# Another order inside the blocks of a fused attention and FFN layer: two chunks' float16 products together, gate ahead of value

## The chip, the cores and the metric

The kernel runs on one core of a Trainium2 chip. The metric is the device time of one execution in microseconds (us); where several executions were timed, the median is given. One execution was also recorded by the hardware profiler. The engines are named as the profile names them: PE (TensorE, matmuls), PEld (its weight loads), DVE (VectorE), ACT (ScalarE), POOL (GpSimd) and SP (SyncE, which only issues transfers here).

## The reference

The layer has 4 x 2048 = 8192 tokens of 256 features, in float32:

```python
Q, K, V = x @ W_q.T, x @ W_k.T, x @ W_v.T
S = (Q_c @ K_c.T) * mask            # in chunks of 32 tokens; mask[i, j] = decay**(i-j) for i >= j
O = S @ V_c
gate = sigmoid(x @ W_g.T)
a = (gate * O) @ W_o.T + x
h = layernorm(x + a)
u = silu(h @ wg.T) * (h @ wu.T)     # wg, wu: 768 x 256 integers / 127
out = layernorm(h + u @ wd.T)       # wd: 256 x 768 integers / 127
```

## The kernel before

The tokens are cut into 16 blocks of 512 (`TB`). One turn of the main loop, `for b in range(NB - 2)`, does the FFN of block b and, between its parts, attention of the blocks after it: `y`, the scores, gate and value of block m = b + 3, and the attention output `o` of block n = b + 2. The order on every engine is written out by hand: `in_turn` (and `in_steady_turn`) keep an instruction in the program's order on its engine. An engine runs its queue in that order; where an instruction waits, everything behind it waits too.

Products are split for precision. Of a projection on attention's side, both operands are cut into float32r pieces, and `three` makes the product in three passes: `hi` x `hi`, then `lo` x `lo` into the same PSUM bank, then ACT scales that bank in place (L542, `nc.scalar.mul(pb, pb, WHOLE)`), and only after that may the third pass, `gap` x `gap`, add to it. The passes stand at L501 where the result is feature by token (`p_y`, `p_g`; 128x512 each) and at L523 where it is token by feature (`p_v`, `p_o`; 128x256 each). The token pieces come from `pieces_of_tokens`: ACT makes `hi` (L472), POOL makes `lo` (L476), DVE makes `gap` (L481). `split_v` ends with an ACT copy of each of its two banks (L576), `split_gate` with a tanh on ACT for each (L559), `split_out` with an addition on DVE (L832).

The FFN's first half, `ffn_up`, runs over six chunks of 128 hidden features. For each it makes four products of 128x512 in float32r (`hi`: `fg_hi` and `fu_hi`, two each) and four in float16 (`lo`), all at L923; ACT takes the silu `s` of the gate bank `fg` (L932), DVE multiplies it with the bank `fu` to `u` (L943), ACT casts `u` to `u_hi` (L948) and POOL makes `u_lo` (L949). Chunks 0, 2 take `hi` first, chunks 1, 3, 4, 5 take `lo` first. With `held=True` the call returns `multiply`, so that other work can be put on the queues ahead of the multiplication.

The second half (`project_back_late`, L764) multiplies `u_hi` with `fd_hi` (float32r, 24 products of 128x256) and then `u_lo` with `fd_lo` (float16, 24). In the blocks with `late = b > 0` its products of chunks 0 and 1 stand between the second and the third pass of `split_out`:

```python
hs[n], out_rest = split_out(n, go_parts)   # passes hi and lo of o, and ACT's two scalings
...
high(range(2))                             # 8 products fdn
mv_h = out_rest()                          # pass gap of o, which needs the scalings
```

So in a block's second half PE's queue reads: chunk 4 of the FFN; value hi, lo; gate hi, lo; value gap; gate gap; chunk 5; o hi, lo; 8 products fdn; o gap; the other fdn. Beside it, in the blocks 1 to 11 (`m + 1 < NB`), the pieces of the next block's tokens are made: ACT's `x_hi` for the two halves k = 0, 1 of the features, DVE's two `x_gap`, POOL's two `x_lo`.

There are 8 PSUM banks of 128x512 float32, and a bank that was let go is taken again by a later product.

Of the kernel before, what the change touches and what calls it, by code (L numbers as in the profile page):

```python
# [58 lines left out]
TB = 512  # L59
# [17 lines left out]
def kernel(  # L77
# [18 lines left out]
    KD = D // P  # L96
# [18 lines left out]
    def in_turn(ins):  # L115
        tc.keep_in_program_order(ins)

    def bank(name):
        return psum.tile([P, TB], F32, tag="ps", name=name)
# [789 lines left out]
        while late_splits:  # L909
            late_splits.pop(0)()  # L910

    def ffn_up(b, hT, uT, chunks, cols=slice(0, TB), held=False, low_first=False):

        n = cols.stop - cols.start
        for hc in chunks:
            pg = bank(f"fg_{b}_{hc}_{cols.start}")[:, :n]
            pu = bank(f"fu_{b}_{hc}_{cols.start}")[:, :n]

            kinds = (1, 0) if hc % 2 or low_first else (0, 1)
            for kind in kinds:  # L920
                for pb, w in ((pg, fg), (pu, fu)):
                    for dc in range(KD):
                        product = nc.tensor.matmul(  # L923
                            pb,
                            lhsT=w[kind][:, dc, hc * P : (hc + 1) * P],
                            rhs=hT[kind][:, dc, cols],
                            start=(kind == kinds[0] and dc == 0),
                            stop=(kind == kinds[1] and dc == KD - 1),
                        )
                        in_turn(product)  # L930
            s = work.tile([P, n], F32, tag="s", name=f"s_{b}_{hc}")
            in_turn(nc.scalar.activation(s, pg, AF.Silu, scale=SCALE / H_UP))  # L932
            no_more_splits()
            if len(uT[0]) == hc:
                for kind, dtype, tiles in zip(("hi", "lo"), (F32R, F16), uT):
                    tiles.append(
                        acts.tile([P, TB], dtype, tag=f"u_{kind}", name=f"u_{kind}_{b}_{hc}")
                    )

            def multiply(hc=hc, pu=pu, s=s):  # L940
                u = work.tile([P, n], F32, tag="u", bufs=3, name=f"u_{b}_{hc}")
                in_steady_turn(
                    nc.vector.scalar_tensor_tensor(u, pu, U_UP / H_UP, s, ALU.mult, ALU.mult)  # L943
                )
                hi, lo = uT[0][hc][:, cols], uT[1][hc][:, cols]

                def split():
                    in_steady_turn(nc.scalar.copy(hi, u))  # L948
                    in_steady_turn(nc.gpsimd.tensor_tensor(lo, u, hi.bitcast(F32), ALU.subtract))  # L949

                if lagging:
                    late_splits.append(split)
                else:
                    split()

            if held:
                return multiply
            multiply()
# [198 lines left out]
    for b in range(NB - 2):  # L1157
        n = b + 2
        m = b + 3
        more = m < NB  # L1160
        xns[n] = load_xn(n)
        if b and m + 1 < NB:
            xTs[m + 1] = load_xT(m + 1)
        hT = hTs.pop(b)
        uT = ([], []) if b else uT_0
        sT, v, sg = ahead
        if not more:
            scales_next = iterated_scale_and_shift(mv_out, of_out, f"out_{b}")
        if b:
            normalize(hs[b + 1], *scales_h)  # L1170
            up_now(b, hT, uT, 0)
        multiply = ffn_up(b, hT, uT, range(1, 2), held=True)
        if b:
            moving = move_h(b + 1, hs[b + 1])
        else:
            cast_fd(0, range(2, 3))
            multiply()
            x_gaps()
            sT = attn_scores(n, yT)
            xTs[m + 1] = load_xT(m + 1)  # L1180
        if more:
            yT, y_rest = split_y(m, x_parts)
        if b:
            multiply()
        if not more:
            goT = attn_values(n, sT, v, sg)
        multiply = ffn_up(b, hT, uT, range(2, 3), held=True)
        if b > 1:
            normalize(r_before, *scales_out, range(NG // 2))
        multiply()  # L1190
        if more:
            y_rest()
        if b == 0:
            normalize(hs[b + 1], *scales_h)
            moving = move_h(b + 1, hs[b + 1])
        if not more:
            go_parts, go_gaps = token_parts(goT, f"go_{n}")
        multiply = ffn_up(b, hT, uT, range(3, 4), held=True)
        if b > 1:
            normalize(r_before, *scales_out, range(NG // 2, NG))  # L1200
        multiply()
        if b > 1:
            store(b - 2, r_before)
        if more:
            sT_next = attn_scores(m, yT)
            goT = attn_values(n, sT, v, sg)
            multiply = ffn_up(b, hT, uT, range(4, 5), held=True, low_first=True)
            go_parts, go_gaps = token_parts(goT, f"go_{n}")
            if b == 0:
                cast_fd(1, range(1))  # L1210
            multiply()
            go_gaps()
            v_next, v_rest = split_v(m, x_parts)
            sg_next, g_rest = split_gate(m, x_parts)
            v_rest()
            late = b > 0
            if late:
                g_rest()
                if m + 1 < NB:
                    x_parts, x_high, x_low, x_difference = pieces_of_tokens(  # L1220
                        xTs[m + 1], f"x_{m + 1}"
                    )
                    x_high(0)
                multiply = ffn_up(b, hT, uT, range(5, 6), held=True)
                if m + 1 < NB:
                    x_high(1)
                    x_difference(0)
                multiply()
                if m + 1 < NB:
                    x_difference(1)  # L1230
            else:
                if b == 0:
                    cast_fd(1, range(1, 2))
                up_with_cast(b, hT, uT, 5, 1, range(2, 3))
        else:
            up_now(b, hT, uT, 4)
            go_gaps()
        r_before = r_out
        if more:
            hs[n], out_rest = split_out(n, go_parts)  # L1240
            if b:
                hTs[b + 1] = split_h(b + 1, moving)
            begun = None
            if late:
                high, low = project_back_late(b, uT, [chunked(w) for w in fd], "fdn")
                high(range(2))
                begun = high, low, range(2, KH)
            else:
                g_rest()
            mv_h = out_rest()  # L1250
            if b == 0:
                hTs[b + 1] = split_h(b + 1, moving)
            ahead = sT_next, v_next, sg_next
            if m + 1 < NB:
                if late:
                    for k in range(KD):
                        x_low(k)
                else:
                    x_parts, x_gaps = token_parts(xTs[m + 1], f"x_{m + 1}")
            std_h = root_in_turn(mv_h, of_h, f"h_{b}")  # L1260
            if b:
                mv_before, std_before = mv_out, root_in_turn(mv_out, of_out, f"out_{b}")
            back_to_silu()

            def between():
                scales = scale_and_shift(
                    mv_h, std_h, of_h, f"h_{b}", nc.vector, in_turn
                )
                if m + 1 < NB and not late:
                    x_gaps()  # L1270
                return scales

            r_out, mv_out, scales_h = ffn_down(b, uT, hs.pop(b), between, begun=begun)
            if b:
                scales_out = scale_and_shift(mv_before, std_before, of_out, f"out_{b}")
        else:
            multiply = ffn_up(b, hT, uT, range(5, KH), held=True)
            hs[n], out_rest = split_out(n, go_parts)
            multiply()
            hTs[b + 1] = split_h(b + 1, moving)  # L1280
            scales_out = scales_next
            normalize(r_before, *scales_out)
            store(b - 1, r_before)

            def amid():
                return iterated_scale_and_shift(out_rest(), (HALF, 1.0), f"h_{n}")

            r_out, mv_out, scales_h = ffn_down(
                b, uT, hs.pop(b), chunkwise=True, amid=amid
            )  # L1290
            scales_out = iterated_scale_and_shift(mv_out, of_out, f"out_{b + 1}")
# [361 lines left out]
```

## Time and profile before

| | |
|---|---|
| time, median of 3 (range) | 485.84 us (485.81 to 486.66) |
| the profiled execution: time, span | 486.48 us, 484.8 us |
| busy: PE, PEld | 478.5 us (99%), 378.6 us (78%) |
| busy: ACT, DVE, POOL | 370.8 us (76%), 348.9 us (72%), 281.5 us (58%) |
| chain that ended last | PE 98% |
| matmuls at L923 (up) | 784, 249 us busy |
| 128x512 up products, hi / lo of fg, mean | 461 / 383 ns |
| 128x256 fdn products, hi / lo, mean | 276 / 273 ns |

Matmuls overlap: the duration of one is longer than its distance to the next one, so what PE needs for a run of products is read from the starts of successive rows and not from durations. The same holds in part for ACT and DVE, where an instruction that needn't wait starts some 0.1 us before the end of the one ahead of it. "x2" behind a row is the number of instructions merged in it, and the second number of a row is then the time from the first one's start to the last one's end.

### The profile page before, as it was taken

How to read it: one execution, taken by the hardware profiler on the slowest of the kernel's cores; microseconds unless marked ns; L12 is line 12 of the kernel's file. 1: busy time of each engine (PE TensorE's matmuls, PEld its weight loads, DVE VectorE, ACT ScalarE, POOL GpSimd, SP SyncE). 2: the span in 40 equal slices, each digit the busy share in tenths (PEclk: the TensorE clock that was granted, in tenths of full speed). 3: DMA queues.
4: the chain of work that ended last, by engine and by line, in shares of the span. 5: the costliest groups of instructions: out<-in, count | busy, mean ns of one | idle time of the engine just before them, and what ended most of it. 6: DMA issues, size and time to landing. Idle time of an engine off the chain costs nothing.

```text
span 484.8 us, 12280 instructions
## 1 busy us (share of the span) xinstructions
PE 478.5 (99%) x4760; PEld 378.6 (78%) x4760; DVE 348.9 (72%) x795; ACT 370.8 (76%) x699; POOL 281.5 (58%) x285
## 2 busy tenths in 40 slices
PE   9999999999999999999999999999999999999995
PEld 5788787787868878687787868878687787868685
DVE  4587958777677776858777677876858777577656
ACT  4778788687888788797887888788797877786845
POOL 2835755655655566455655654566455655657764
PEclk9999999999999999999999999999999999999999
DMA  8630321211313114031321313114031211103102
GB/s 258 233 96 26 112 64 46 71 62 34 105 51 119 44 41 137 25 107 49 93 79 33 108 52 117 45 45 131 26 108 50 83 45 35 56 19 114 35 16 83
DMA packets 43323, 36.99 MB, mean 76 GB/s; under 512 B 4864, under 2 KB 39168, under 8 KB 43264
## 3 DMA queue, kind: packets, MB, share of 16 engines
q1 hardware_dynamic: 42144, 35.28, 23.6%
q10 hardware_dynamic: 1120, 0.92, 0.6%
q8 instruction: 38, 0.62, 0.5%
q14 instruction: 21, 0.17, 0.1%
HBM read 20.45 MB, written 8.39 MB: 59 GB/s over the span
## 4 chain that ended last, share of the span: by engine, by line
PE 98%; DMA 1%; DVE 0%; ACT 0%; issue 0%
PE fg L923 18%; PE fu L923 18%; PE fdn L764 13%; PE p_v L523 9%; PE p_y L501 9%; PE p_o L523 9%; PE p_g L501 9%; PE po L699 4%; PE ps L663 2%; PE fdn L1001 2%; PE fdn L1395 1%; PE fdn L745 1%; PE pg L587 1%; PE pa L811 1%; PE pv L629 1%; DMA wg<-in_w_gT_dram 1%
## 5 line engine op out<-in xcount | busy, mean ns | idle before, releaser
L949 POOL TENSOR_TENSOR u_lo<-u,u_hi 128x512 f16<-128x512 f32 (+1 forms) x98 | 129.6, 1329 | 92.7 <-ACT u_hi L948 92.7
L943 DVE SCALAR_TENSOR_TENSOR u<-fu,s 128x512 f32<-128x512 f32 (+1 forms) x98 | 66.1, 675 | 46.8 <-ACT s L932 44.8
L932 ACT ACTIVATE s<-fg 128x512 f32<-128x512 f32 (+1 forms) x98 | 57.5, 587 | 34.2 <-PE fg L923 33.3
L948 ACT CAST u_hi<-u 128x512 fp32r<-128x512 f32 (+1 forms) x98 | 59.5, 607 | 31.2 <-DVE u L943 31.2
L923 PE MATMUL fg<-hT_hi,fg_hi 128*128 128x512 f32 (+1 forms) x196 | 73.1, 454 | 0.0
L923 PE MATMUL fu<-hT_hi,fu_hi 128*128 128x512 f32 (+1 forms) x196 | 60.3, 389 | 0.0
L923 PE MATMUL fg<-hT_lo,fg_lo 128*128 128x512 f16 (+1 forms) x196 | 58.2, 379 | 0.0
L923 PE MATMUL fu<-hT_lo,fu_lo 128*128 128x512 f16 (+1 forms) x196 | 57.4, 375 | 0.0
L476 POOL TENSOR_TENSOR go_lo<-goT,go_hi 128x512 fp32r<-128x512 f32 x30 | 44.6, 1506 | 18.5 <-ACT go_hi L472 18.5
L481 DVE SCALAR_TENSOR_TENSOR go_gap<-go_hi,goT 128x512 fp32r<-128x512 f32 x30 | 48.3, 1647 | 0.8 <-ACT go_hi L472 0.7
L476 POOL TENSOR_TENSOR x_lo<-xT,x_hi 128x512 fp32r<-128x512 f32 x30 | 37.6, 1273 | 15.2 <-ACT x_hi L472 15.2
L923 PEld LDWEIGHTS fg<-hT_hi,fg_hi 128*128 128x128 f32 x196 | 35.6, 190 | 10.3
L923 PEld LDWEIGHTS fu<-hT_hi,fu_hi 128*128 128x128 f32 x196 | 36.5, 188 | 8.2
L481 DVE SCALAR_TENSOR_TENSOR x_gap<-x_hi,xT 128x512 fp32r<-128x512 f32 x30 | 21.9, 740 | 27.2 <-ACT x_hi L472 27.2
L900 POOL TENSOR_TENSOR hT_lo<-hT,hT_hi 128x512 f16<-128x512 f32 x28 | 35.7, 1295 | 4.6 <-ACT hT_hi L899 4.6
L832 DVE TENSOR_TENSOR h<-p_o,x 128x512 f32<-128x512 f32 x30 | 19.3, 685 | 25.3 <-PE p_o L523 23.2
L764 PE MATMUL fdn<-fd_hi,u_hi 128*128 128x256 f32 x288 | 36.5, 276 | 0.0
L923 PEld LDWEIGHTS <-fu_lo 128*128 128x128 f16 x196 | 19.2, 98 | 22.1
L764 PEld LDWEIGHTS fdn<-fd_hi,u_hi 128*128 128x128 f32 x288 | 34.4, 188 | 0.0
L764 PE MATMUL fdn<-fd_lo,u_lo 128*128 128x256 f16 x288 | 33.5, 273 | 0.0
L923 PEld LDWEIGHTS <-fg_lo 128*128 128x128 f16 x196 | 13.2, 98 | 21.8 <-issue 16.1
L764 PEld LDWEIGHTS <-u_lo 128*128 128x128 f16 x288 | 27.2, 98 | 3.4
(179 smaller groups left out, 1065.7 us busy)
## 6 DMA issues: line engine op xcount, KB each, us to landing
x<-in_x_dram SPq DMA_DIRECT2D x16, 512.0 KB, 3.8
xT<-in_xT_dram SPq DMA_DIRECT2D x15, 512.0 KB, 4.3
hT<-sq SPq DMA_DIRECT2D x224, 32.0 KB, 1.9
out_dram<-r SPq DMA_DIRECT2D x13, 512.0 KB, 3.3
out_dram<-r SPq DMA_DIRECT2D x7, 128.0 KB, 1.7
fg_int<-in_ffn_gT_dram SPq DMA_DIRECT2D x3, 256.0 KB, 7.3
fu_int<-in_ffn_uT_dram SPq DMA_DIRECT2D x3, 256.0 KB, 6.4
fd_int<-in_ffn_dT_dram SPq DMA_DIRECT2D x3, 256.0 KB, 5.5
```

Source lines behind the costliest of these rows:

```text
L476: in_turn(nc.gpsimd.tensor_tensor(lo[:, k, :], t[:, k, :], whole, ALU.subtract))
L481: nc.vector.scalar_tensor_tensor(gap[:, k, :], whole, -WHOLE, t[:, k, :], ALU.mult, ALU.add)
L501: nc.tensor.matmul(pb, lhsT=a[kind][:, k, i * P : (i + 1) * P], rhs=b[kind][:, k, :], start=kind + k == 0, stop=True, skip_group_check=True,)
L523: nc.tensor.matmul(pb[:, j * D : (j + 1) * D], lhsT=b[kind][:, k, g * P : (g + 1) * P], rhs=a[kind][:, k, :], start=kind + k + j == 0, sto ...
L699: product = nc.tensor.matmul(po[dims, dc * len(groups) + g, :], lhsT=v[rows, g, dc * P + dims.start : dc * P + dims.stop], rhs=sT[rows, g, :],
L764: nc.tensor.matmul(banks[g // per][:, g % per * D : (g % per + 1) * D], lhsT=part[:, g * P : (g + 1) * P], rhs=w, start=first and g % per ...
L900: nc.gpsimd.tensor_tensor(in_order[1], whole, in_order[0].bitcast(F32), ALU.subtract)
L923: product = nc.tensor.matmul(pb, lhsT=w[kind][:, dc, hc * P : (hc + 1) * P], rhs=hT[kind][:, dc, cols], start=(kind == kinds[0] and dc == ...
L932: in_turn(nc.scalar.activation(s, pg, AF.Silu, scale=SCALE / H_UP))
L943: nc.vector.scalar_tensor_tensor(u, pu, U_UP / H_UP, s, ALU.mult, ALU.mult)
L948: in_steady_turn(nc.scalar.copy(hi, u))
L949: in_steady_turn(nc.gpsimd.tensor_tensor(lo, u, hi.bitcast(F32), ALU.subtract))
```

## The change

The blocks 1 to 12 get another order; block 0 and the last three are left as they were.

- Chunks 0 and 1: all eight float16 products first, then the eight float32r products.
- Chunk 3: `hi` first instead of `lo` first.
- Chunks 4 and 5: the eight float16 products together, then chunk 4's float32r ones. Chunk 5's float32r products are moved behind the gate's third pass and ahead of the value's.
- Gate is made ahead of value.
- ACT's order behind that: the two tanh, the silu of chunk 5, the two copies of `v`, both `x_high`. Then `x_difference(0)` on DVE, then chunk 5's multiplication (DVE) with its cast (ACT), then `x_difference(1)`. Before, `x_high(0)` stood ahead of that silu and `x_high(1)` behind it, and `x_difference(0)` was also ahead of the multiplication.

`ffn_up` is cut into `ffn_pieces`, which gives the float32r products, the float16 products and the activation of one chunk as three functions. The number of instructions of each kind is unchanged.

```diff
@@ -909,25 +909,30 @@
         while late_splits:
             late_splits.pop(0)()
 
-    def ffn_up(b, hT, uT, chunks, cols=slice(0, TB), held=False, low_first=False):
+    def ffn_pieces(b, hT, uT, hc, cols=slice(0, TB)):
 
         n = cols.stop - cols.start
-        for hc in chunks:
-            pg = bank(f"fg_{b}_{hc}_{cols.start}")[:, :n]
-            pu = bank(f"fu_{b}_{hc}_{cols.start}")[:, :n]
-
-            kinds = (1, 0) if hc % 2 or low_first else (0, 1)
-            for kind in kinds:
-                for pb, w in ((pg, fg), (pu, fu)):
-                    for dc in range(KD):
+        pg = bank(f"fg_{b}_{hc}_{cols.start}")[:, :n]
+        pu = bank(f"fu_{b}_{hc}_{cols.start}")[:, :n]
+        fresh = [pg, pu]
+
+        def products(kind):
+            for i, (pb, w) in enumerate(((pg, fg), (pu, fu))):
+                for dc in range(KD):
+                    for part in [cols]:
                         product = nc.tensor.matmul(
-                            pb,
+                            pb[:, part.start - cols.start : part.stop - cols.start],
                             lhsT=w[kind][:, dc, hc * P : (hc + 1) * P],
-                            rhs=hT[kind][:, dc, cols],
-                            start=(kind == kinds[0] and dc == 0),
-                            stop=(kind == kinds[1] and dc == KD - 1),
+                            rhs=hT[kind][:, dc, part],
+                            start=len(fresh) > 1 - i,
+                            stop=True,
+                            skip_group_check=True,
                         )
                         in_turn(product)
+                        if len(fresh) > 1 - i:
+                            fresh.pop()
+
+        def activate():
             s = work.tile([P, n], F32, tag="s", name=f"s_{b}_{hc}")
             in_turn(nc.scalar.activation(s, pg, AF.Silu, scale=SCALE / H_UP))
             no_more_splits()
@@ -937,7 +942,7 @@
                         acts.tile([P, TB], dtype, tag=f"u_{kind}", name=f"u_{kind}_{b}_{hc}")
                     )
 
-            def multiply(hc=hc, pu=pu, s=s):
+            def multiply():
                 u = work.tile([P, n], F32, tag="u", bufs=3, name=f"u_{b}_{hc}")
                 in_steady_turn(
                     nc.vector.scalar_tensor_tensor(u, pu, U_UP / H_UP, s, ALU.mult, ALU.mult)
@@ -953,6 +958,17 @@
                 else:
                     split()
 
+            return multiply
+
+        return lambda: products(0), lambda: products(1), activate
+
+    def ffn_up(b, hT, uT, chunks, cols=slice(0, TB), held=False, low_first=None):
+
+        for hc in chunks:
+            high, low, activate = ffn_pieces(b, hT, uT, hc, cols)
+            for products in (low, high) if (hc % 2 if low_first is None else low_first) else (high, low):
+                products()
+            multiply = activate()
             if held:
                 return multiply
             multiply()
@@ -1166,10 +1182,25 @@
         sT, v, sg = ahead
         if not more:
             scales_next = iterated_scale_and_shift(mv_out, of_out, f"out_{b}")
+        late = more and b > 0
+
+        def pieces(hc):
+            return ffn_pieces(b, hT, uT, hc)
+
         if b:
             normalize(hs[b + 1], *scales_h)
-            up_now(b, hT, uT, 0)
-        multiply = ffn_up(b, hT, uT, range(1, 2), held=True)
+        if late:
+            (high_0, low_0, silu_0), (high_1, low_1, silu_1) = pieces(0), pieces(1)
+            low_0()
+            low_1()
+            high_0()
+            silu_0()()
+            high_1()
+            multiply = silu_1()
+        else:
+            if b:
+                up_now(b, hT, uT, 0)
+            multiply = ffn_up(b, hT, uT, range(1, 2), held=True)
         if b:
             moving = move_h(b + 1, hs[b + 1])
         else:
@@ -1195,7 +1226,7 @@
             moving = move_h(b + 1, hs[b + 1])
         if not more:
             go_parts, go_gaps = token_parts(goT, f"go_{n}")
-        multiply = ffn_up(b, hT, uT, range(3, 4), held=True)
+        multiply = ffn_up(b, hT, uT, range(3, 4), held=True, low_first=not late)
         if b > 1:
             normalize(r_before, *scales_out, range(NG // 2, NG))
         multiply()
@@ -1204,33 +1235,40 @@
         if more:
             sT_next = attn_scores(m, yT)
             goT = attn_values(n, sT, v, sg)
-            multiply = ffn_up(b, hT, uT, range(4, 5), held=True, low_first=True)
-            go_parts, go_gaps = token_parts(goT, f"go_{n}")
-            if b == 0:
-                cast_fd(1, range(1))
-            multiply()
-            go_gaps()
-            v_next, v_rest = split_v(m, x_parts)
-            sg_next, g_rest = split_gate(m, x_parts)
-            v_rest()
-            late = b > 0
             if late:
+                (high_4, low_4, silu_4), (high_5, low_5, silu_5) = pieces(4), pieces(5)
+                low_4()
+                low_5()
+                go_parts, go_gaps = token_parts(goT, f"go_{n}")
+                high_4()
+                silu_4()()
+                go_gaps()
+                sg_next, g_rest = split_gate(m, x_parts)
+                v_next, v_rest = split_v(m, x_parts)
                 g_rest()
+                high_5()
+                multiply = silu_5()
+                v_rest()
                 if m + 1 < NB:
                     x_parts, x_high, x_low, x_difference = pieces_of_tokens(
                         xTs[m + 1], f"x_{m + 1}"
                     )
-                    x_high(0)
-                multiply = ffn_up(b, hT, uT, range(5, 6), held=True)
-                if m + 1 < NB:
-                    x_high(1)
+                    for k in range(KD):
+                        x_high(k)
                     x_difference(0)
                 multiply()
                 if m + 1 < NB:
                     x_difference(1)
             else:
-                if b == 0:
-                    cast_fd(1, range(1, 2))
+                multiply = ffn_up(b, hT, uT, range(4, 5), held=True, low_first=True)
+                go_parts, go_gaps = token_parts(goT, f"go_{n}")
+                cast_fd(1, range(1))
+                multiply()
+                go_gaps()
+                v_next, v_rest = split_v(m, x_parts)
+                sg_next, g_rest = split_gate(m, x_parts)
+                v_rest()
+                cast_fd(1, range(1, 2))
                 up_with_cast(b, hT, uT, 5, 1, range(2, 3))
         else:
             up_now(b, hT, uT, 4)
```

## The prediction

> **What bounds the kernel now.** First the page's head and its chain of the work that ended last, then what PE waited for between 90 and 420 us, where twelve blocks repeat every 29.07 us (in the chain's rows, value begins at 148.72 and 177.78).
>
> ```profile
> PE 478.5 (99%) x4760; PEld 378.6 (78%) x4760; DVE 348.9 (72%) x795; ACT 370.8 (76%) x699; POOL 281.5 (58%) x285
> PEclk9999999999999999999999999999999999999999
> PE 98%; DMA 1%; DVE 0%; ACT 0%; issue 0%
> ```
>
> PE is the chain, at full granted clock, and in that stretch the list of PE's waits is empty. So only two things move the time: the pace of PE's products, and a wait that PE doesn't have now. For both I read one block's second half, engine by engine. PE first (start, time from first start to last end, engine, line, product):
>
> ```profile
> 154.07 0.60 PE L923 MATMUL fg<-hT_lo,fg_lo 128*128 128x512 f16 x2
> 154.51 0.59 PE L923 MATMUL fu<-hT_lo,fu_lo 128*128 128x512 f16 x2
> 154.76 0.82 PE L923 MATMUL fg<-hT_hi,fg_hi 128*128 128x512 f32 x2
> 155.41 0.62 PE L923 MATMUL fu<-hT_hi,fu_hi 128*128 128x512 f32 x2
> 155.87 0.64 PE L523 MATMUL p_o<-wo_hi,go_hi 128*128 128x256 f32 x4
> 157.71 1.07 PE L764 MATMUL fdn<-fd_hi,u_hi 128*128 128x256 f32 x8
> 158.62 1.07 PE L523 MATMUL p_o<-wo_gap,go_gap 128*128 128x256 f32 x8
> ```
>
> The last row is the one to watch: o's third pass, which needs ACT's scaling of the bank. ACT and DVE in the same stretch:
>
> ```profile
> 152.95 1.08 ACT L576 COPY v<-p_v 128x512 f32<-128x512 f32 x2
> 153.92 1.10 ACT L559 ACTIVATE sg<-p_g 128x512 f32<-128x512 f32 x2
> 154.88 0.65 ACT L472 ACTIVATE x_hi<-xT 128x512 fp32r<-128x512 f32 x1
> 155.61 0.60 ACT L932 ACTIVATE s<-fg 128x512 f32<-128x512 f32 x1
> 156.11 0.62 ACT L472 ACTIVATE x_hi<-xT 128x512 fp32r<-128x512 f32 x1
> 157.02 0.62 ACT L948 CAST u_hi<-u 128x512 fp32r<-128x512 f32 x1 [0.29 <-DVE u L943]
> 157.55 1.06 ACT L542 ACTIVATE p_o<-p_o 128x512 f32<-128x512 f32 x2
> ...
> 155.57 0.69 DVE L481 SCALAR_TENSOR_TENSOR x_gap<-x_hi,xT 128x512 fp32r<-128x512 f32 x1 [2.47 <-ACT x_hi L472]
> 156.30 0.69 DVE L943 SCALAR_TENSOR_TENSOR u<-fu,s 128x512 f32<-128x512 f32 x1
> 156.91 0.68 DVE L481 SCALAR_TENSOR_TENSOR x_gap<-x_hi,xT 128x512 fp32r<-128x512 f32 x1
> ```
>
> The first scaling ends at 157.55 + 0.58 (a single one's length, from the p_g row below) = 158.13, and PE begins the third pass at 158.62. That 0.49 us, less what handing over takes, is all the room there is today. The scaling stands behind the cast of u, the cast behind u on DVE, and u behind the first x_gap: a queue of three engines in step.
>
> **The change, part one: fewer changes of product type on PE.** From start to start the four float16 products of one chunk go at 0.22 us each (two fg in 154.51 - 154.07 = 0.44). Float32r products inside a long run go at 0.23 (p_y, 168.04 to 169.41: six in 1.37). By ends of single products, the float16 ones are 216 ns apart and long-run float32r ones 229; the first float16 product behind float32r ends 230 behind it, 14 more than its like; four float32r ones behind float16 take 929 to 936 instead of 4 x 229 = 916, some 16 more. A switch to float16 and back therefore costs 0.030 us.
>
> Per block: with chunks 0 and 1 one switch pair goes (float16 now follows fdn's own float16): 0.030. With 4 and 5 another: 0.030. With chunk 3 hi first, its float32r joins p_y's third pass and the scores follow float16, a neighbour that no row shows; the return is saved (0.016) unless the scores pay it, so 0 to 0.03. Gate ahead of value exchanges neighbours of one type: 0, within 0.01. Sum 0.06 to 0.09, I take 0.076, times 12 blocks = 0.9 us saved.
>
> [...]
>
> **Part two: where the room goes.** Call E the end of the value's last gap product, now the last thing ahead of o. Chunk 5's float32r products stand 8 gap products (0.92 us) ahead of E, so its silu is done in time. But ACT now has four instructions between that silu and the cast, and the first two wait for the value's gap:
> - The second v copy can start at E + 0.04 (an ACT instruction follows PE by 0.04: p_g's lo ends at 152.39, its scaling starts at 152.43).
> - x_hi(0) starts 0.49 later (spacing of the pairs in the ACT rows): E + 0.53, ends at + 0.65: E + 1.18. x_hi(1) follows and is no further burden.
> - x_gap(0) on DVE 0.03 later (155.53 to 155.57): E + 1.21.
> - u of chunk 5 is behind it: 0.61 later (156.30 to 156.91): E + 1.82, ends at E + 2.51. s and fu were ready long before; it waits only for its turn.
> - u_hi 0.03 later, E + 2.54; the scaling of p_o 0.53 later (157.02 to 157.55), E + 3.07, ends at E + 3.65.
> - PE follows ACT after 0.05: E + 3.70. That spacing is from an early wait, rows below: the scalings start at 64.14, the first ends at 64.72, PE at 64.77.
>
> ```profile
> 152.43 0.58 ACT L542 ACTIVATE p_g<-p_g 128x512 f32<-128x512 f32 x1 [0.34 <-PE p_g L501]
> 64.14 1.06 ACT L542 ACTIVATE p_v<-p_v 128x512 f32<-128x512 f32 x2
> 64.77 1.22 PE L523 MATMUL p_v<-wv_gap,x_gap 128*128 128x256 f32 x8
> ```
>
> PE's own way: o's first product starts 0.16 before the end of the one ahead of it (fu_hi ends at 155.41 + 0.62 = 156.03, p_o starts at 155.87), o's 16 products take 157.71 - 155.87 = 1.84, the 8 of fdn 158.62 - 157.71 = 0.91. So PE is at the third pass at E + 2.59. It waits 3.70 - 2.59 = 1.11 us, where it had 0.49 to spare. A product that starts from a wait took 0.11 longer (387 ns at 64.77, 278 for the next), so 1.22 per block. Behind the waiting product in PE's queue is all the rest of the block, so nothing covers it.
>
> The second bank's scaling ends at E + 3.07 + 1.06 = E + 4.13 and PE gets there 4 products later, at E + 4.27: no second wait. What else is later by this: u_lo of chunk 5, then hT_lo twice, then x_lo twice on POOL (1.29, 2.55, some 2.5), from E + 3.24. hT_lo is ready at about E + 7.1, and the next block's float16 products, which now come first, start behind o's gap, 16 fdn hi and 24 lo at about E + 9.1. No wait there. The two chunks that go together hold four of the eight PSUM banks at once; the last to come free for chunk 5 is one that the silu of chunk 3 reads (0.60 from 173.73), some 2 us before it is wanted, and fdn's two are those of the gate, free after the tanh, 3 us before. In the first half the silu of chunk 0 is asked for later, but its u stands behind DVE's statistics in any case, and y's scaling (0.58 from 169.74, third pass at 171.02) has 0.6 to spare: no cost taken.
>
> Only blocks with a next block to prepare have x_hi: 1 to 11. 11 x 1.22 = 13.4. With 0.9 saved the sum is + 12.5. On the profiled execution: span 484.8 + 12.5 = 497.3, with the 1.7 around it 499.0. The median of the runs lies 0.64 below that execution, so 498.3.
>
> Bounds: without the restart and with 0.05 less on each side of the handoffs the wait is 1.0; with 0.05 more on three handoffs 1.35. That is 11.0 to 14.9, less 0.5 to 1.4 saved: 495.4 to 500.2.
>
> **The rivals.**
> - Not slower: the room holds, PE never waits and only the switches count, 485.84 - 0.9 = 484.9; if they are worth twice as much, 484.0. It decides on one place, the scaling of p_o: the queue of E + 3.70 must shrink to E + 2.59, as it would if both x_hi ran ahead of the v copies (2 x 0.5 us). For: ACT has idle time in the block and xT has landed long before. Against: the written order holds each engine. 5 in 100, of which 3 within 0.2%.
> - DVE takes u ahead of x_gap(0). Then the cast follows x_hi(1) at E + 1.55, the scaling E + 2.08, PE at 2.71: a wait of 0.12 + 0.11, 11 x 0.23 - 0.9 = + 1.6, 487.4. Against: the difference is called first. 4 in 100.
> - x_gap(0) also slows down: beside POOL's work DVE's same instruction took 1.78 (go_gap at 151.31) against 0.69. 11 x 1.09 more: 510.3. Against: POOL's u_lo of chunk 4 is done 3 us before, and its next work needs this very cast. 3 in 100.
>
> **How the numbers follow.** The forecast has 88 in 100, and 498.3 is its time. The range 495.4 to 500.2 holds nearly all of it and none of the rivals. What a measurement here can tell from no change is about 0.2%, 1.0 us: faster 0.02, same 0.03, slower 0.95.
>
> **What would show it.** Right: PE's waits show p_o at L523 (or the line it has then) waiting for ACT's p_o, 11 times, 1.0 to 1.2 each; in that stretch ACT shows v x2, x_hi x2, u_hi, p_o in one row; the distance of the blocks grows from 29.07 to about 30.2; block 12 has no such wait. Switches right: blocks' PE work shorter by 0.06 to 0.09. Wrong: no PE wait at the third pass of o, or x_gap far from 0.69, or a wait at the first float16 products of a block, which I take as covered.

## The result, and the profile after

The changed kernel takes 501.4 us (median of 5, 501.24 to 501.81) against 485.84 before: 1.032 times as long (95% interval 1.030 to 1.033). The direction, and the place and the mechanism of the larger part of the loss, were forecast; a second wait was not. The loss is 15.6 us where 12.5 were forecast, and 501.4 lies 1.2 above the range. The profiled execution took 501.81 us with a span of 500.1, 15.3 more than before.

The page's head and chain of the changed kernel:

```profile
PE 482.2 (96%) x4760; PEld 383.3 (77%) x4760; DVE 348.0 (70%) x795; ACT 371.8 (74%) x699; POOL 275.4 (55%) x285
PEclk9999999999999999999999999999999999999999
PE 88%; ACT 5%; DVE 4%; issue 1%; DMA 1%; ACTq 0%; DVEq 0%
```

The granted clock is still full and PE is busy for only 3.7 us more, but the chain now leaves PE for ACT and DVE in 9% of the span. The list of PE's waits over the whole span (who waited for whom: us in total, times, longest) says where:

```profile
PE p_o L523 <- ACT p_o L542: 11.4, 11, 1.0
PE pi L197 <- PEq L1676: 1.0, 1, 1.0
PE ps L663 <- DVE yT L567: 0.2, 1, 0.2
```

Eleven waits of o's third pass, one per block with a next block to prepare. The second row is in both kernels, at the start. The third is new and was not forecast. One block's second half by engine, the changed kernel's PE, then ACT, then DVE:

```profile
157.81 1.09 PE L523 MATMUL p_v<-wv_gap,x_gap 128*128 128x256 f32 x8
160.55 1.07 PE L764 MATMUL fdn<-fd_hi,u_hi 128*128 128x256 f32 x8
162.66 1.23 PE L523 MATMUL p_o<-wo_gap,go_gap 128*128 128x256 f32 x8 [1.04 <-ACT p_o L542]
163.73 1.98 PE L764 MATMUL fdn<-fd_hi,u_hi 128*128 128x256 f32 x16
...
158.54 1.08 ACT L576 COPY v<-p_v 128x512 f32<-128x512 f32 x2 [0.33 <-PE p_v L523]
159.50 1.17 ACT L472 ACTIVATE x_hi<-xT 128x512 fp32r<-128x512 f32 x2
161.50 0.62 ACT L953 CAST u_hi<-u 128x512 fp32r<-128x512 f32 x1 [0.84 <-DVE u L948]
162.03 1.06 ACT L542 ACTIVATE p_o<-p_o 128x512 f32<-128x512 f32 x2
...
160.18 0.69 DVE L481 SCALAR_TENSOR_TENSOR x_gap<-x_hi,xT 128x512 fp32r<-128x512 f32 x1 [3.44 <-ACT x_hi L472]
160.79 0.68 DVE L948 SCALAR_TENSOR_TENSOR u<-fu,s 128x512 f32<-128x512 f32 x1
```

Read it as a relay. Value's gap products end at E = 157.81 + 1.09 = 158.90. Then come the copies of v, x_hi, x_gap, u, u_hi and the scaling of p_o, each row starting where the one it needs has ended, and PE at 162.66. ACT's cast notes its own 0.84 us of idleness, put down to DVE's u. PE by itself would have been at the third pass 0.91 behind 160.55, at 161.46.

What a block costs PE in parts, in us (sums of the distances between the ends of successive products, in a typical block; "best" is the last experiment):

| part | before | after | best |
|---|---|---|---|
| o, third pass | 0.907 | 2.262 | 0.907 |
| scores (ps) | 0.692 | 0.79 | 0.693 |
| up, float16 | 5.346 | 5.316 | 5.316 |
| up, float32r | 5.561 | 5.527 | 5.530 |
| o, first two passes | 1.840 | 1.813 | 1.813 |
| y, third pass | 0.932 | 0.915 | 0.915 |
| whole block | 29.067 | 30.40 | 28.953 |

So 11 x 1.355 = 14.9 us are lost at o's third pass. The scores lose some 0.10 in each of eleven blocks (0.08 to 0.11) and 0.35 more in one of them, 1.43 together. The fewer switches save 0.108 per block, 12 x 0.108 = 1.3. That makes 15.0 of the 15.3 us; the other 0.3 are small irregularities of single blocks and of the start.

### The profile page after: what moved, and what is told of

Same layout as the page of the kernel before. It is cut to its first block, busy times and chain, and to the rows that moved or that the text cites. A ratio compares the mean times of both kernels' runs of the same rounds, so it can differ in the third digit from the quotient of the medians.

```text
span 500.1 us, 12280 instructions
## 1 busy us (share of the span) xinstructions
PE 482.2 (96%) x4760; PEld 383.3 (77%) x4760; DVE 348.0 (70%) x795; ACT 371.8 (74%) x699; POOL 275.4 (55%) x285
## 4 chain that ended last, share of the span: by engine, by line
PE 88%; ACT 5%; DVE 4%; issue 1%; DMA 1%; ACTq 0%; DVEq 0%
PE fg L923 17%; PE fu L923 17%; PE fdn L764 11%; PE p_g L501 8%; PE p_y L501 8%; PE p_v L523 7%; PE p_o L523 5%; PE po L699 4%; PE ps L663 2%; ACT v L576 2%; PE fdn L1017 2%; DVE x_gap L481 2%; DVE u L948 1%; ACT p_o L542 1%; ACT x_hi L472 1%
## 5 line engine op out<-in xcount | busy, mean ns | idle before, releaser
L923 PE MATMUL fg<-hT_hi,fg_hi 128*128 128x512 f32 (+1 forms) x196 | 67.4, 425 | 0.0
L476 POOL TENSOR_TENSOR go_lo<-goT,go_hi 128x512 fp32r<-128x512 f32 x30 | 39.3, 1332 | 14.5 <-ACT go_hi L472 14.5
L476 POOL TENSOR_TENSOR x_lo<-xT,x_hi 128x512 fp32r<-128x512 f32 x30 | 37.5, 1271 | 15.3 <-ACT x_hi L472 15.3
L481 DVE SCALAR_TENSOR_TENSOR go_gap<-go_hi,goT 128x512 fp32r<-128x512 f32 x30 | 45.1, 1541 | 0.8 <-ACT go_hi L472 0.7
L472 ACT ACTIVATE go_hi<-goT 128x512 fp32r<-128x512 f32 x30 | 17.3, 624 | 22.5 <-DVE goT L718 22.5
```

The costliest lines, as they stand in the source:

```text
L472: in_turn(nc.scalar.mul(hi[:, k, :], t[:, k, :], TOP))
L476: in_turn(nc.gpsimd.tensor_tensor(lo[:, k, :], t[:, k, :], whole, ALU.subtract))
L481: nc.vector.scalar_tensor_tensor(gap[:, k, :], whole, -WHOLE, t[:, k, :], ALU.mult, ALU.add)
L923: product = nc.tensor.matmul(pb[:, part.start - cols.start : part.stop - cols.start], lhsT=w[kind][:, dc, hc * P : (hc + 1) * P], rhs=hT[k ...
```

## The experiments

The diffs of the first four experiments are against the changed kernel. Four theories were to be told apart. **Q**: the queue of ACT and DVE ahead of p_o's scaling makes the wait at o. **N**: the loss is PE's own, from the new order of products or banks wanted too early. For the scores' small loss, **P**: DVE's chain to yT comes later because POOL's x_lo does; **S**: the scores are dearer behind float16 products.

### u ahead of the first x_gap

```diff
                     for k in range(KD):
                         x_high(k)
-                    x_difference(0)
                 multiply()
                 if m + 1 < NB:
-                    x_difference(1)
+                    for k in range(KD):
+                        x_difference(k)
```

> The changed kernel, with chunk 5's multiplication put ahead of x_difference(0) on DVE; nothing else moves. Theory Q (the queue: PE waits at o's third pass because its scaling stands on ACT behind two v copies, two x_hi and the cast of u, and u on DVE behind the first x_gap): u no longer waits for x_gap, so the cast follows x_hi(1) on ACT. From E, the end of the value's gap products (158.90 in the changed kernel's profile), x_hi(1) starts at E + 1.13, the cast 0.51 later, the scaling 0.53 later at E + 2.17, PE at E + 2.80 instead of the E + 3.76 seen. The third pass, 2.26 us of PE per block now, falls by 0.96 to about 1.3, and the time by 11 x 0.96 = 10.5 to 490.9 (490 to 492). Rival N (neighbours: what was lost is PE's own pace or a bank that the new order of products wants too early): order on DVE does not matter to it; 501.4 stays within 1 us.

Measured: 490.74 us (ratio to before 1.0095, interval 1.008 to 1.011). The third pass takes 1.315 per block. One swap of two DVE instructions gives back 10.7 us: N is out for the bulk. What is left, this kernel's PE and ACT show:

```profile
158.61 1.07 PE L764 MATMUL fdn<-fd_hi,u_hi 128*128 128x256 f32 x8
159.77 1.23 PE L523 MATMUL p_o<-wo_gap,go_gap 128*128 128x256 f32 x8
...
159.12 1.08 ACT L542 ACTIVATE p_o<-p_o 128x512 f32<-128x512 f32 x2
```

PE could start at 158.61 + 0.91 = 159.52 and starts at 159.77. The list of waits doesn't name it: the last fdn product is recorded as ending at 159.68, so only 0.09 us show as idle. The distance of the starts has the whole 0.25.

### Both x_hi ahead of the copies of v

```diff
+                if m + 1 < NB:
+                    x_parts, x_high, x_low, x_difference = pieces_of_tokens(
+                        xTs[m + 1], f"x_{m + 1}"
+                    )
+                    for k in range(KD):
+                        x_high(k)
                 v_rest()
                 if m + 1 < NB:
...
-                    for k in range(KD):
-                        x_high(k)
                     x_difference(0)
```

> The changed kernel, with both x_high put ahead of the two v copies on ACT (behind chunk 5's silu); x_difference(0) still ahead of the multiplication. Theory Q: x_gap(0) can start when the value's gap products have read the old one, E + 0.05; u E + 0.66, the cast E + 1.37, the scaling E + 1.90, PE at E + 2.53, just where it arrives by itself (E + 2.56). No wait at o's third pass, or under 0.1. The time is then 485.8 less the switches (0.105 per block by the table of both profiles, 12 blocks: 1.3) plus what the second, small wait costs, the one of the scores for yT (0.10 per block now): 484.6 to 487.0. Rival N: 501.4 stays within 1 us.

Measured: 488.58 us (1.0055, 1.0042 to 1.0068), 1.6 above the top of what was expected. The third pass is at 1.08, not 0.91: 11 x 0.17 = 1.9 us. The release does come just when PE arrives:

```profile
157.23 1.07 PE L764 MATMUL fdn<-fd_hi,u_hi 128*128 128x256 f32 x8
158.16 1.22 PE L523 MATMUL p_o<-wo_gap,go_gap 128*128 128x256 f32 x8
...
157.53 1.06 ACT L542 ACTIVATE p_o<-p_o 128x512 f32<-128x512 f32 x2
```

PE is there at 157.23 + 0.91 = 158.14 and starts at 158.16, but the eight products take 1.22 instead of 1.07. A release that is late by some 0.02 costs 0.17. In the kernel before, the weight load of each of these products starts 0.11 ahead of the product; in the changed kernel, and here, the first one's starts together with its product, held by the same wait. Counted from where that weight load could have started, the release is late by 0.13. The third pass's products in one block (min/median/max ns), in the kernel before:

```profile
L523 PE MATMUL p_o<-wo_gap,go_gap x8: 276/276/276, 158.6 to 159.4; 128*128 128x256 f32 x8
```

and in the changed kernel:

```profile
L523 PE MATMUL p_o<-wo_gap,go_gap x8: 277/283/384, 162.7 to 163.6; 128*128 128x256 f32 x8
```

The first one is 108 ns longer and the next seven some 7 each.

### x_hi and u both ahead

```diff
+                if m + 1 < NB:
+                    x_parts, x_high, x_low, x_difference = pieces_of_tokens(
+                        xTs[m + 1], f"x_{m + 1}"
+                    )
+                    for k in range(KD):
+                        x_high(k)
+                multiply()
                 v_rest()
                 if m + 1 < NB:
...
-                        x_high(k)
-                    x_difference(0)
-                multiply()
-                if m + 1 < NB:
-                    x_difference(1)
+                        x_difference(k)
```

> The changed kernel, with ACT's order silu of chunk 5, both x_hi, the cast of u, both v copies, and u ahead of both x_gap on DVE. Theory Q: the scaling starts at E + 1.75, PE could go at E + 2.38 and arrives at E + 2.56: 0.18 to spare, no wait. Time as for the kernel with only x_high moved or up to 1 us less: 484.6 to 486.5. If the scores' small wait is set by how late POOL's x_lo runs (theory P), it is some 0.1 to 0.2 per block here as well, since the scaling, the casts of hT and with them POOL's queue are 0.25 later against PE than in the kernel before: then nearer to 486. Rival N: 501.4.

Measured: 486.29 us (1.0004, 0.9995 to 1.0013). From the second of these blocks on, the third pass is back at 0.907, all of it; in the first it takes 1.17. But the scores stay at 0.77 to 0.79, and the switches' gain is not to be seen in the time.

### POOL's x_lo early, in the changed kernel

```diff
                     for k in range(KD):
                         x_high(k)
+                        x_low(k)
                     x_difference(0)
...
-                if late:
-                    for k in range(KD):
-                        x_low(k)
-                else:
+                if not late:
                     x_parts, x_gaps = token_parts(xTs[m + 1], f"x_{m + 1}")
```

> The changed kernel, with POOL's two x_lo taken from behind hT_lo and put right behind their x_hi, ahead of u_lo of chunk 5; all else as changed. Theory P (the scores wait for yT because DVE's minus_h, 0.9 to 1.2 us for 4 elements, ends with POOL's last x_lo, 0.42 later against PE than before, and residual, u of chunk 0 and yT queue behind it): minus_h falls to some 0.2 us, the scores' 0.79 per block returns to 0.69, the one block with 1.14 too; o's third pass stays at 2.26 or gets up to 0.7 worse if an x_lo holds up the first x_gap. 501.4 - 11 x 0.10 - 0.35 = 500.0. Rival S (the scores cost more because they now follow float16 products): the scores stay at 0.79 and the time at 501.4 within 0.5.

Measured: 500.42 us. The scores are at 0.69 in all eleven blocks while o's third pass stays at 2.26: P holds, and S falls, since the scores still follow float16 products here. The link is visible on POOL and DVE. In the kernel before:

```profile
161.72 2.51 POOL L476 TENSOR_TENSOR x_lo<-xT,x_hi 128x512 fp32r<-128x512 f32 x2
163.34 0.92 DVE L388 TENSOR_SCALAR minus_h<-rstd_h 128x4 f32<-128x4 f32 x1
```

In the changed kernel:

```profile
166.20 2.49 POOL L476 TENSOR_TENSOR x_lo<-xT,x_hi 128x512 fp32r<-128x512 f32 x2
167.51 1.20 DVE L388 TENSOR_SCALAR minus_h<-rstd_h 128x4 f32<-128x4 f32 x1
```

minus_h handles four elements per partition. It ends 0.02 to 0.03 behind the last x_lo in both (164.26 to 164.23, 168.71 to 168.69). With x_lo moved its median is 0.17 us. Behind it on DVE stand the residual, the statistics, u of chunk 0, the transposes and, at last, the two copies of yT. x_lo itself is later against PE because it follows o's scaling, by way of the casts of hT: that scaling starts 1.07 ahead of the third pass before and only 0.63 ahead after. The end of this chain, DVE's copies and PE's scores, in the kernel before:

```profile
172.54 1.28 DVE L567 COPY yT<-p_y 128x512 f32<-128x512 f32 x2
174.03 0.76 PE L663 MATMUL ps<-yT,xT 128*32 128x32 f32 x64
```

In the changed kernel:

```profile
177.00 1.28 DVE L567 COPY yT<-p_y 128x512 f32<-128x512 f32 x2
178.17 0.85 PE L663 MATMUL ps<-yT,xT 128*32 128x32 f32 x64
```

Counted from the start of o's third pass, x_lo ends at 5.61 before and at 6.02 after, and the last copy of yT at 15.20 and 15.61: the same 0.41 later. The scores come at 15.41 and 15.51. Their first eight products start before the second copy has ended; the ninth waits for it. In the kernel before, the ninth starts 0.29 behind that copy's end; in the changed kernel it starts 0.06 behind it, in all eleven blocks.

The Trainium skill has this in "SBUF — State Buffer", section "SBUF: two separate sides": VectorE and GpSimd share a pair of ports that one instruction holds to its end, against a VectorE instruction in a two-port mode or with two inputs in SBUF. That minus_h ends with an x_lo in every block that has one, and takes 0.17 beside an idle POOL, agrees with it; in which mode minus_h runs, no row shows.

### The halves of the change by themselves

Second half alone (against the changed kernel: chunks 0, 1 and 3 as before):

```diff
-        if late:
-            (high_0, low_0, silu_0), (high_1, low_1, silu_1) = pieces(0), pieces(1)
...
-            multiply = silu_1()
-        else:
-            if b:
-                up_now(b, hT, uT, 0)
-            multiply = ffn_up(b, hT, uT, range(1, 2), held=True)
+        if b:
+            up_now(b, hT, uT, 0)
+        multiply = ffn_up(b, hT, uT, range(1, 2), held=True)
...
-        multiply = ffn_up(b, hT, uT, range(3, 4), held=True, low_first=not late)
+        multiply = ffn_up(b, hT, uT, range(3, 4), held=True)
```

> The kernel before with the second half of the change alone: chunks 4 and 5, gate ahead of value, and the new order on ACT and DVE; chunks 0, 1 and 3 as they were. Theory Q: the wait at o's third pass is all there, 2.26 us of PE per block against 0.91, 11 x 1.355 = 14.9 more; the switches of this half save 0.057 per block (chunk 4 and 5, and o's first products). The scores' wait for yT is smaller than in the whole change, since PE gets to them 0.05 later in the first half: 0 to 0.07 per block. 485.9 + 14.9 - 0.7 + 0 to 0.8 = 500.1 to 500.9. Rival N (the first half's order of products carries a part of the loss): well below 500.

Measured: 501.51 us (1.0322, 1.0307 to 1.0337), the whole loss, and 0.6 above the top of the expected. The third pass is at 2.26; the scores at 0.73 to 0.77 in all blocks but one, though they follow float32r products. So the first half brings nothing in the changed kernel: its 0.05 per block turns into a longer wait for yT.

First half alone (in the changed kernel, the lines from chunk 4 to the difference of the pieces are those of before):

```diff
             if late:
-                (high_4, low_4, silu_4), (high_5, low_5, silu_5) = pieces(4), pieces(5)
-                low_4()
-                low_5()
...
+                g_rest()
...
+                    x_high(0)
+                multiply = ffn_up(b, hT, uT, range(5, 6), held=True)
...
+                    x_high(1)
+                    x_difference(0)
```

> The kernel before with the first half of the change alone: the float16 products of chunks 0 and 1 together, chunk 3 float32r first. Theory Q: no wait at o. Theory P: x_lo runs as early as it did before, so yT has its old 0.15 us to spare at the scores, of which this saves PE 0.06: no wait there either, the scores stay at 0.69. Saved per block about 0.06 (two switches to float16 or back in chunks 0 and 1, one return in y's third pass), 12 x 0.06 = 0.7: 485.2, which is within what can be told from no change. Rival S (scores behind float16 products cost 0.1): 0.79 for the scores and 485.9 or more.

Measured: 485.46 us, ratio 0.9988 (0.998 to 0.9997). The scores are at 0.69 and a block at 28.993: 0.074 less than before.

### A control, and the best of both

The kernel before, with x_lo early alone:

```diff
                     x_high(0)
+                    x_low(0)
...
                     x_high(1)
+                    x_low(1)
                     x_difference(0)
...
-                if late:
-                    for k in range(KD):
-                        x_low(k)
-                else:
+                if not late:
```

> The kernel before with one edit alone: POOL's two x_lo right behind their x_hi instead of behind hT_lo. A control: PE waits for nothing there, so POOL's order should change nothing: 485.9 within 0.3. If an x_lo that holds up x_gap(0), and so u and the scaling, by more than the 0.43 to spare shows, the third pass of o gets longer and the time up to 0.5 x 11 = 5 worse.

Measured: 486.04 us (1.0004, 0.9995 to 1.0012), a block 29.067 as before. yT is ready 0.2 earlier there, and nobody waits for it: the move is worth something only where that wait exists.

x_hi, u and x_lo all ahead (the edits of the third and the fourth experiment together; shown is what comes on top of the third, less the lines that take x_lo out of its old place):

```diff
                     for k in range(KD):
                         x_high(k)
+                        x_low(k)
                 multiply()
                 v_rest()
```

> The kernel with x_hi and u ahead (both_ahead), and POOL's x_lo right behind x_hi as well. Both waits should be gone: third pass of o at 0.91, scores at 0.69. What is left of the change is the switches alone, 29.07 - 0.105 = 28.96 us per block: 485.9 - 1.3 = 484.6. If theory P is wrong and the scores' cost belongs to the order of the products: 486.3 as without x_lo moved.

Measured: 485.04 us, ratio 0.9979 (0.997 to 0.9988), 0.9 us faster than the kernel before. Its o, on PE and ACT:

```profile
157.71 1.07 PE L764 MATMUL fdn<-fd_hi,u_hi 128*128 128x256 f32 x8
158.62 1.07 PE L523 MATMUL p_o<-wo_gap,go_gap 128*128 128x256 f32 x8
...
157.78 1.12 ACT L542 ACTIVATE p_o<-p_o 128x512 f32<-128x512 f32 x2
```

The third pass follows fdn at 0.91 as before the change, from the second of these blocks on (1.17 in the first), and the list of PE's waits has no row of o and none of the scores. A typical block is 28.953, 0.114 less than before, so what the switches save is all there. The collision of DVE with POOL is not gone but moved: beside the early x_lo the two x_gap take 1.69 and 1.78 us in a typical block, where the kernel before has 0.68 to 0.69. Here u stands ahead of them, and PE does not wait for it.

## Why the prediction was right or wrong

**Where the time goes: right.** The relay from value's gap products to p_o's scaling was worked out from rows of before, with each handoff in its order, and came to E + 3.70; it is E + 3.76. PE's own arrival was put at E + 2.59 and is E + 2.56. The number of blocks (11), PE waiting at L523 for ACT's L542, and block 12 without such a wait were as said.

**The term per block: too small.** 1.22 forecast, 1.355 measured. The gap of 1.11 is 1.20: x_hi starts at E + 0.60 instead of E + 0.53, behind a second v copy that starts at E + 0.12 and not at E + 0.04, every handoff behind it is as forecast, and PE is there 0.03 earlier. The restart of 0.11 is 0.16: only the first product's lengthening had been counted, not that the seven behind it go slower too. 0.135 x 11 = 1.5 us of the miss.

**The first half: wrong.** "No cost taken" was the step that failed. It looked at silu, u of chunk 0 and y's scaling, and not at yT's copies and the scores behind them, where the kernel before has only some 0.24 us to spare (the second copy ends at 173.82, the ninth score product starts at 174.11, less 0.05 for handing over). It also took what is later on POOL as harmless because each of its products was in time; x_lo was in time, but DVE's minus_h did not end until x_lo had, and yT came 0.41 later against PE. Put at 0, it measured 1.43 us. The long go_gap beside go_lo, which a rival of the forecast used, looks like the same effect, and it was sought in the wrong place.

**The switches: right, slightly low.** 0.076 per block forecast, 0.108 measured, 0.4 us over the twelve blocks. The first two passes of o, which now stand straight behind value's float32r products and no longer behind a chunk that has just changed type, gain 0.027, which had not been counted; the open neighbour, scores behind float16, costs nothing (the fourth experiment has 0.69 there). The saving shows by itself in the blocks of the last experiment, 0.114 shorter than before with no wait of o or the scores.

The sum: 1.5 + 1.43 - 0.4 = 2.5 of the 3.1 us by which 501.4 exceeds 498.3. Another 0.2 is that the median lies 0.41 below the profiled execution and not 0.64. The rest is not assigned; the irregularities named above and the spread of the runs are as large. The range was made from the one wait's handoffs alone. The measured 1.355 per block is just at its upper bound of 1.35; a bound for a second wait was missing, and by the sum it is the scores' 1.43 that carry the time past 500.2. The fourth experiment, without that wait, took 500.42 (499.82 to 500.75), too near to 500.2 to confirm this alone.

**The rivals.** That DVE takes u first was priced at 487.4 and takes 490.74, for the same reasons: ACT's x_hi(1) later, the restart dearer, the scores' wait. That both x_hi ahead of the v copies would take the wait away comes close: the release is then 0.02 late, but the restart and the scores' wait are still paid, and the time is 488.58 and not 484.9. x_gap(0) takes 0.69 in the changed kernel, as the forecast had it; beside an early x_lo it does slow down, as the last experiment shows.

## What to carry to other kernels

When products are put in a new order on the engine that bounds the kernel, write down for every product that waits how far ahead its release comes, and redo that list for the new order with each helper engine's queue; here 0.1 us saved per block cost 1.4 because a copy that used to be early was now the last thing ahead of four others. Move the helpers' instructions along with the products: the short ones that feed PE first, the ones that only prepare the next block behind them. A gain that arrives at the next wait only lengthens that wait, so the wait has to be moved as well, and the release must come before PE is there: in the first experiment it came 0.25 us too late and cost 0.41, in the second 0.02 and cost 0.17. After such a move look again at what now runs side by side: with x_lo moved, minus_h was short again, but the two x_gap took over 1 us longer each.

## What the runs showed that was not expected

- A float32r product that has to wait costs some 0.15 to 0.16 us on top of the wait, over eight products of 128x256: its weight load, which otherwise starts 0.11 ahead, is held too. This is so even when the release is late by only 0.02.
- A DVE instruction on 4 elements per partition took 0.92 (before) to 1.22 us (after) beside POOL's subtraction of 512 and 0.17 without, and ended 0.02 to 0.03 behind it each time.
- In one of the eleven blocks of the changed kernel DVE's residual started 0.36 later than in the others for nothing that the profile shows, and the scores waited that much longer (1.14 for 0.79). The same shows in two of the experiments. Its cause stays open.
